# Fetching the rows of B and C three states ahead, in buffers that also take the second group's products

## The chip, the core and the metric

The kernel runs on one core of a Trainium2 chip. Five engines of that core work beside each other, each through its own queue in order: TensorE (PE in the profile, with its weight loads as PEld), VectorE (DVE), ScalarE (ACT), GpSimd (POOL) and SyncE (SP), which here only issues transfers. They meet through semaphores. The metric is the device time of one execution in microseconds. Before the change it is 2395.06 us, the median of three runs (2393.68 to 2396.68).

## The reference

4096 tokens (2 x 2048) of 256 features go through three layers, each added to its input:

```python
x = x + 0.5 * ffn(layernorm(x))      # 8 experts of 256 -> 1024 -> 256, top 2, capacity 640 per choice
x = x + mamba_block(layernorm(x))    # the block below
x = x + 0.5 * ffn(layernorm(x))      # the same experts again
```

The middle block is a state space layer and a small squared-ReLU network. Its core is a recurrence over time for 512 channels with 16 states each:

```python
xz = rmsnorm(x) @ in_proj_w.T;  x_in, z = split(xz)
u  = silu(causal_conv4(x_in));  x_dbl = u @ x_proj_w.T          # -> dt_low (64), B (16), C (16)
dt = softplus(dt_low @ dt_proj_w.T + dt_proj_b);  A = -exp(A_log)
h  = h * exp(dt_t * A) + (dt_t * u_t) * B_t                     # per step, 512 x 16 values
y  = sum over the 16 states of h * C_t
out = ((y + u * D) * silu(z)) @ out_proj_w.T
```

B and C have 16 rows each, one per state, and every channel uses the same row.

## The kernel before, in words

**Three stages.** `moe1` (to about 620 us in the profile) and `moe2` (from about 1996 us) run the two expert layers in units of 256 gathered tokens; they are matmuls with small work beside them. `mamba` lies between. The expert units that `moe1` leaves over ("b", four units) and those of the second expert layer that can start early ("c", four units) run beside the recurrence.

**The recurrence** (`recurrence`, L1345). Tokens are cut into 8 chunks of 512. Channels lie on the 128 partitions in 4 groups, which are taken in pairs (`PR = 2`). One slot k is one state s of one group c of one chunk: `order` (L1352) runs chunk, pair, state, and innermost the two groups of the pair, so there are 512 slots, and two neighbouring slots use the same row of B and the same row of C. `divmod(k, PR)` gives the state slot n and the group q (0 or 1) in it. For each slot:

- `load(n)` (L1359), once per state slot: SP fetches row s of B into `bt` (L1366) and row s of C into `ct` (L1367), each spread over all 128 partitions, 256 KB.
- `drive(k)` (L1369): POOL multiplies dt x u (`dtu`) by `bt` into `db` (L1380), three slots ahead.
- `decay(k)` (L1382): ACT computes exp(dt x A) into a PSUM bank `h`, two slots ahead.
- `scan(k)` (L1390): DVE runs the scan over 512 steps in that bank (L1396), and ACT copies the last column as the next chunk's start, `st` (L1401).
- `output(k)` (L1403), one slot later: DVE multiplies `h` by `ct` into `hc` (L1406), and PE adds it to the group's sum in PSUM through an identity matmul (L1417). The first state of a pair also adds u x D (L1411); after the last one `gate` (L1420) multiplies with silu(z).

**Buffers.** Each is 128 x 512 values of 4 bytes. There are 2 of `bt` and 4 of `ct` in pool "bc", and 4 of `db` and 5 of `hc` in pool "scan": 15 in all. A new tile waits for the last reader of the tile that had its buffer.

**Order of the rest.** All other work of the block is written as generators that yield a `Need`: modelled times on engines, a PSUM bank, a mark to wait for. `Side` plans them: after each slot, `slot` (L152) adds the slot's own times (`OWN`) to a modelled busy time of each engine and emits whichever steps fit. `AHEAD` says how far an engine's modelled time may run past that of the slot before the model moves the slot, `BEHIND` how late an engine may be and still be given another step, and `late` how long after a step its result is there. `until(mark)` (L166) emits steps, the earliest first, until a mark is set: `drive` uses it for the step sizes of a pair (mark "dt") and `load` for the rows of B and C (mark "bc").

`chunk_front` (L1147) prepares a chunk: it fetches x (L1155), normalises (`bn`, L1165), projects, convolves, computes B and C, stores them to DRAM (`bc`, L1261), from which `load` reads them, and then dt and dtu (`steps`, `log1p`, last op L1308). `chunk_tail` (L1451) finishes one: it fetches x once more as `xt` (L1459), takes ACT's `v` from it (L1480), projects out, runs the small network, stores the result to `out` (L1517) and calls `route` (L389), the routing of the second expert layer. `route` normalises (`bn`, POOL's `nmr`, ACT's `row`, L421) and stores the 512 KB of rows to one or two DRAM buffers (L429): two for the first four chunks, one for the others. All these fetches and stores are issued from SP, whose queue also carries the loads of B and C.

Of the kernel before, what the change touches and what calls it, by code (L numbers as in the profile page):

```python
# [9 lines left out]
F32 = mybir.dt.float32  # L10
# [3 lines left out]
ALU = mybir.AluOpType  # L14
# [5 lines left out]
B, T, D = 2, 2048, 256  # L20
# [13 lines left out]
RW = D + 2  # L34
# [5 lines left out]
NU_A, NU_B, NU_C, NU_D = 28, 4, 7, 25  # L40
# [34 lines left out]
class Side:  # L75
# [4 lines left out]


    OWN = {"dve": 1.8, "act": 0.88, "pe": 0.0, "pool": 1.27}
    BEHIND = {"dve": 0.6, "act": 1.2, "pe": 4.0, "pool": 4.0}
    AHEAD = {"dve": 0.0, "act": 2.0, "pe": 4.5, "pool": 4.0}
    EARLY = {"dve": 0.4, "act": 0.8, "pe": 1.0, "pool": 1.0}

    def __init__(self):
# [141 lines left out]
class Kernel:  # L229
# [156 lines left out]

        self.nc.gpsimd.tensor_tensor(out, in_, self.nhalf[:, : in_.shape[1]], ALU.pow)

    def route(self, x, t0, pool, bank, rows, pair=None):  # L389


        nc = self.nc
        n = x.shape[1]
# [24 lines left out]
        row = t("row", [P, n, RW])  # L418
        for j in range(n):
            yield Need(act=0.45)  # L420
            nc.scalar.activation(  # L421
                row[:, j, :D], x[:, j, :], AF.Identity,
                bias=nmr[:, j : j + 1], scale=rstd[:, j : j + 1],
            )

        def store(a, columns):
            for to in rows:
                at = to[t0 * P : (t0 + n) * P, columns].rearrange("(j p) d -> p j d", p=P)
                nc.sync.dma_start(out=at, in_=a)  # L429

        if pair is None:
            lg = t("lg")
        else:
            store(row[:, :, :D], slice(0, D))
            if j1 == 0:
                pair["lg"] = t("lg", [P, 2 * n, E])
            lg = pair["lg"]
# [32 lines left out]
        size, gates = n, row[:, :, D:]  # L470
        if pair is not None:
# [88 lines left out]
        at, late = t("at", W3), t("late", W3)  # L560
        nc.vector.scalar_tensor_tensor(at, best, float(PB), blk, ALU.mult, ALU.add)
        nc.vector.tensor_scalar(late, pos, float(CAP), SKIP, ALU.is_ge, ALU.mult)
        nc.vector.tensor_tensor(at, at, late, ALU.add)
        store(row if pair is None else gates, slice(0 if pair is None else D, RW))
        for j in range(0, n, size):
            yield from self.enlist(t, bank, lo[:, j : j + size], at[:, j : j + size], t0 + j)

# [579 lines left out]
    def chunk_front(self, i, pools, ch, before):  # L1147

        nc = self.nc
        pool, stp, ps, dr = pools["work"], pools["state"], pools["ps"], pools["dram"]  # L1150
        W1 = [P, TC]
        v, g, act = nc.vector, nc.gpsimd, nc.scalar
        yield Need(late=2.5, after=("b", NU_B - 1 if i == NCHUNK // 2 else -1))
        x = pool.tile([P, NJ, D], F32, tag="x", name="x")
        nc.sync.dma_start(out=x, in_=self.tiles(self.acc)[i])  # L1155

# [92 lines left out]
        NR = DTR + 2 * DS  # L1249
# [7 lines left out]
        xd = pool.tile(W1, F32, tag="xd", name="xd")[:NR, :]  # L1257
        yield Need(act=0.6, free=1, sets=("bc", i))
        act.copy(xd, xp)
        bc = ch["bc"] = dr.tile([2 * DS, TC], F32, tag="bc", name="bc")  # L1260
        nc.sync.dma_start(out=bc[:, :], in_=xd[DTR:NR, :])  # L1261


        yield self.log1p(i, pool, ch)
# [80 lines left out]
    def recurrence(self, pools, chunks, side):  # L1345

        nc = self.nc
        sp, bcp, stp = pools["scan"], pools["bc"], pools["state"]  # L1350
        W1 = [P, TC]
        order = [  # L1352
            (i, p * PR + q, s) for i in range(NCHUNK) for p in range(NP) for s in range(DS)
            for q in range(PR)
        ]
        pairs = order[::PR]
        dA, db, bt, ct, y, h, hc = {}, {}, {}, {}, {}, {}, {}

        def load(n):  # L1359
            if n < len(pairs):  # L1360
                i, _, s = pairs[n]
                side.until(("bc", i))
                bt[n] = bcp.tile(W1, F32, tag="bt", name="bt")
                ct[n] = bcp.tile(W1, F32, tag="ct", name="ct", bufs=4)
                bc = chunks[i]["bc"]
                nc.sync.dma_start(out=bt[n], in_=bc[s : s + 1, :].partition_broadcast(P))  # L1366
                nc.sync.dma_start(out=ct[n], in_=bc[DS + s : DS + s + 1, :].partition_broadcast(P))  # L1367

        def drive(k):  # L1369
            if k < len(order):  # L1370
                i, c, s = order[k]
                n, q = divmod(k, PR)
                if q == 0:
                    if s == 0:
                        side.until(("dt", NC * i + c + PR - 1))
                    if n == 0:
                        load(n)
                    load(n + 1)
                db[k] = sp.tile(W1, F32, tag="db", name="db", bufs=4)
                nc.gpsimd.tensor_tensor(db[k], chunks[i]["dtu"][c // PR][:, q, :], bt[n], ALU.mult)  # L1380

        def decay(k):  # L1382
            if k < len(order):
                i, c, s = order[k]
                dA[k] = pools["h"].tile(W1, F32, tag="h", name="h")
                nc.scalar.activation(  # L1386
                    dA[k], chunks[i]["dt"][c], AF.Exp, scale=self.A[:, c, s : s + 1]
                )

        def scan(k):  # L1390
            i, c, s = order[k]
            ch = chunks[i]
            if k % (NC * DS) == 0:
                ch["state"] = stp.tile([P, NC, DS], F32, tag="st", name="st")
            h[k] = dA.pop(k)
            nc.vector.tensor_tensor_scan(  # L1396
                h[k], h[k], db.pop(k),
                chunks[i - 1]["state"][:, c, s : s + 1] if i % (T // TC) else 0.0,
                ALU.mult, ALU.add,
            )  # L1400
            nc.scalar.copy(ch["state"][:, c, s : s + 1], h[k][:, TC - 1 :])  # L1401

        def output(k):  # L1403
            i, c, s = order[k]
            t = hc[k] = sp.tile(W1, F32, tag="hc", name="hc", bufs=5)
            nc.vector.tensor_tensor(t, h.pop(k), ct[k // PR], ALU.mult)  # L1406
            if k % (PR * DS) < PR and k >= PR:
                gate(k - PR)
            if s == 0:
                y[c] = pools["yps"].tile(W1, F32, tag="y", name="y_ps")  # L1410
                nc.tensor.matmul(  # L1411
                    y[c], lhsT=self.skip[:, c, :], rhs=chunks[i]["xc"][c], start=True, stop=False
                )
                side.did(pe=0.88)
                if k % PR == PR - 1:
                    side.mark(("begun", NP * i + c // PR))
            nc.tensor.matmul(y[c], lhsT=self.ident, rhs=hc.pop(k), start=False, stop=(s == DS - 1))  # L1417
            side.did(pe=0.88)

        def gate(k):  # L1420
            i, c, _ = order[k]
            ch = chunks[i]
            side.until(("out", i - 1))
            yc = ch["yc"][c] = pools["work"].tile(W1, F32, tag="yc", name="yc", bufs=4)
            side.until(("z", NC * i + c))
            nc.vector.tensor_tensor(yc, y[c], ch["zs"][c], ALU.mult)
            side.did(dve=0.68)
            if k % PR == PR - 1:
                side.mark(("scan", NP * i + c // PR))

        for k in range(3):
            drive(k)
        self.lone = False
        while self.lent:
            side.earliest()
        for k in range(2):
            decay(k)
        for k in range(len(order) + 1):
            if k < len(order):
                scan(k)  # L1440
                decay(k + 2)
            if k:
                output(k - 1)
            drive(k + 3)
            side.mark(("slot", k))
            side.slot()
        self.lone = True
        for k in range(len(order) - PR, len(order)):
            gate(k)

    def chunk_tail(self, i, pools, ch):  # L1451

        nc = self.nc
        pool, ps = pools["work"], pools["ps"]
        g, W1 = nc.gpsimd, [P, TC]
        y = ch["yc"]
        yield Need(late=2.5, rank=1)
        x = pool.tile([P, NJ, D], F32, tag="xt", name="xt")
        nc.sync.dma_start(out=x, in_=self.tiles(self.acc)[i])  # L1459
        yield Need(after=("scan", NP * i + NP - 1))  # L1460
# [32 lines left out]
        t = pool.tile([P, NJ], F32, tag="rs_in", name="rs_in")  # L1493
# [20 lines left out]
            yield Need(act=0.6)  # L1514
            nc.scalar.activation(hm[:, c, :], hm[:, c, :], AF.Square)
        yield from pairs(lambda c: hm[:, c, :], self.w_pr, "pr_ps", x, x)
        nc.sync.dma_start(out=self.tiles(self.out)[i], in_=x)  # L1517
        yield Need()
        half = i < NCHUNK // 2
        to = self.rows[1:] if half else self.rows[1:2]  # L1520
        if i % 2 == 0:
            self.pair = {}
        yield from self.route(x, i * NJ, pool, lambda tag: (ps, "mm"), to, self.pair)
        yield Need(sets=("routed", i))
        if i == NCHUNK // 2 - 1:
            yield self.plan_half(pools["exp"])
# [3 lines left out]
    def mamba(self):  # L1530
# [3 lines left out]
        with ExitStack() as ctx:  # L1534
# [5 lines left out]
            def aside(name, bufs):  # L1540
                tp = tc.tile_pool(name=f"mb_{name}", bufs=bufs, side="right")
                return short.enter_context(tp)

            pools = {
                "scan": aside("scan", 2),
                "bc": aside("bc", 2),
                "work": pool("work", 1),
                "exp": pool("exp", 1),
                "state": pool("state", 2),
# [105 lines left out]
```

## Time and profile before

| | us |
|---|---|
| median of three runs | 2395.06 |
| the profiled execution | 2385.7 |
| its span in the trace | 2384.0 |
| first to last slot of the recurrence | 641 to 1862 |
| in these 1221 us: PE / DVE / ACT / POOL busy | 1061 / 1075 / 734 / 911 |

The profile is one execution. Its page gives the busy time of each engine and, for forty equal slices of the span, busy shares in tenths; PEclk is the TensorE clock that was granted, as a share of full speed. Groups of instructions are named by line, engine and tile: "h<-h,st,db" of L1396 is the scan. A line of waits says which engine's instruction waited for which other one: total us, how often, the longest. A timeline line gives start, duration, engine, line, operation and, in brackets, the engine's idle time before it and what ended it. "SPq" is SP's queue; its instructions are the issues of transfers, which land some time after.

### The profile page before, as it was taken

The numbers are of one execution on the slowest core, as the hardware profiler recorded it, in microseconds if no ns is written. First come the engines' busy times: TensorE is split into PE (matmuls) and PEld (weight loads), VectorE is DVE, ScalarE is ACT, GpSimd is POOL, SyncE is SP. The second block draws the span as 40 slices with busy tenths as digits, with TensorE's granted clock in tenths as the row PEclk, the third lists the DMA queues.
The fourth block names the chain that finished last, engine by engine and source line by source line (L and its number), as shares of the span: only waits on it lengthen the run. The fifth ranks groups of instructions, "written<-read, shape, count | busy, mean of one in ns | idle before, by whom it ended". The sixth has DMA issues, their size and how long they took to land. (4 is left out here: it accounts for less than half of the span.)

```text
span 2384.0 us, 24140 instructions
## 1 busy us (share of the span) xinstructions
PE 2058.1 (86%) x7253; PEld 1309.4 (55%) x7253; DVE 1339.1 (56%) x2321; ACT 1018.7 (43%) x2316; POOL 1467.8 (62%) x1408
## 2 busy tenths in 40 slices
PE   4399999977798898997989877899888986999997
PEld 2288888864453343442434433344445665888886
DVE  6521112111287897989988898899988342111111
ACT  4122222212556666766576653676645321222221
POOL 3355555543687877877688764877767436555543
PEclk8599999998899998999999987999989998999999
DMA  8165544652264454444455434454455334565463
GB/s 265 57 223 153 155 115 115 186 156 65 66 167 121 124 139 138 126 142 113 137 133 143 128 95 135 131 143 132 114 137 157 92 95 131 187 191 152 117 192 104
DMA packets 155625, 326.14 MB, mean 137 GB/s; under 512 B 30387, under 2 KB 77340, under 8 KB 147804
## 3 DMA queue, kind: packets, MB, share of 16 engines
q1 hardware_dynamic: 115868, 174.17, 26.3%
q0 software_dynamic: 39616, 150.31, 21.3%
q8 instruction: 61, 1.00, 0.2%
q14 instruction: 80, 0.66, 0.1%
HBM read 324.86 MB, written 36.38 MB: 152 GB/s over the span
## 5 line engine op out<-in xcount | busy, mean ns | idle before, releaser
L1380 POOL TENSOR_TENSOR db<-dtu,bt 128x512 f32<-128x512 f32 x512 | 653.4, 1306 | 199.9 <-DVE h L1396 100.1
L1417 PE MATMUL y_ps<-hc,ident 128*128 128x512 f32 x1024 | 557.7, 652 | 121.6 <-DVE hc L1406 121.2
L1396 DVE TENSOR_TENSOR_SCAN h<-h,st,db 128x512 f32<-128x512 f32 x384 | 491.0, 1279 | 30.7 <-POOL db L1380 26.4
L800 ACT ACTIVATE h<-hp,w 128x256 f32<-128x256 f32 x424 | 178.0, 471 | 644.9 <-PE hp L842 584.2
L1417 PEld LDWEIGHTS y_ps<-hc,ident 128*128 128x128 f32 x1024 | 189.5, 201 | 396.0 <-DVE hc L1406 256.3
L842 PE MATMUL hp<-xbT,w 128*128 128x256 f32 x1696 | 378.0, 381 | 10.0 <-DMA w<-in_expert,widxd 3.0
L849 PE MATMUL yp<-w,h 128*128 128x256 f32 x1696 | 376.7, 380 | 0.0
L1386 ACT ACTIVATE h<-dt,A 128x512 f32<-128x512 f32 x512 | 358.9, 701 | 2.7 <-POOL dt L1306 2.3
L1406 DVE TENSOR_TENSOR hc<-h,ct 128x512 f32<-128x512 f32 x512 | 344.1, 672 | 27.2 <-ACT st L1401 27.0
L842 PEld LDWEIGHTS hp<-xbT,w 128*128 128x128 f32 x1696 | 321.5, 191 | 61.1 <-issue 7.3
L849 PEld LDWEIGHTS yp<-w,h 128*128 128x128 f32 x1696 | 319.7, 191 | 41.7
L785 DVE COPY xbT<-tp 128x512 f32<-128x512 f32 x53 | 36.7, 692 | 374.0 <-PE tp L781 374.0
L1401 ACT COPY st<-h 128x1 f32<-128x1 f32 x512 | 81.2, 159 | 352.6 <-DVE h L1396 351.6
L811 DVE TENSOR_TENSOR y<-yp,w 128x256 f32<-128x256 f32 x106 | 45.0, 425 | 288.0 <-PE yp L849 288.0
L763 POOL DMA_INDIRECT acc<-y,ids x56 | 90.3, 1612 | 152.9 <-DMA acc<-y,ids 68.8
L1396 DVE TENSOR_TENSOR_SCAN h<-h,db 128x512 f32<-128x512 f32 x128 | 156.2, 1220 | 34.6 <-POOL db L1380 31.9
L763 POOL DMA_INDIRECT out<-y,ids x50 | 80.0, 1600 | 144.1 <-DMA out<-y,ids 69.9
L196 POOL DMA_INDIRECT xb<-rows,ids x128 | 134.7, 1052 | 40.9 <-issue 33.0
L1326 PE MATMUL in_ps<-rT,w_in 128*128 128x512 f32 x256 | 126.8, 621 | 2.4 <-DVE zs L1321 1.4
L1212 PE MATMUL cv_ps<-xpad,taps 128*128 128x512 f32 x256 | 120.1, 594 | 1.3 <-DVE zs L1321 0.8
L842 PE MATMUL e_hp<-e_xT,w 128*128 128x256 f32 x352 | 90.7, 408 | 13.6 <-DVE e_y L948 8.0
L842 PEld LDWEIGHTS e_hp<-e_xT,w 128*128 128x128 f32 x352 | 72.2, 208 | 38.2 <-issue 11.3
(318 smaller groups left out, 2366.8 us busy)
## 6 DMA issues: line engine op xcount, KB each, us to landing
bt<-bc SPq DMA_DIRECT2D x256, 256.0 KB, 3.7
ct<-bc SPq DMA_DIRECT2D x256, 256.0 KB, 4.4
rows<-row SPq DMA_DIRECT2D x12, 512.0 KB, 3.3
w<-in_expert SPq DMA_DIRECT2D x2, 2304.0 KB
x<-in_x SPq DMA_DIRECT2D x8, 512.0 KB, 4.6
acc<-x SPq DMA_DIRECT2D x8, 512.0 KB, 5.2
xt<-acc SPq DMA_DIRECT2D x8, 512.0 KB, 5.9
x<-acc SPq DMA_DIRECT2D x8, 512.0 KB, 4.2
```

The lines of the kernel that those rows point to most:

```text
L196: self.nc.gpsimd.indirect_dma_start(out=out, out_offset=None, in_=src, in_offset=bass.IndirectOffsetOnAxis(ap=idx, axis=0), bounds_check=l ...
L763: self.nc.gpsimd.indirect_dma_start(out=dst, out_offset=bass.IndirectOffsetOnAxis(ap=ids, axis=0), in_=y, in_offset=None, bounds_check=las ...
L800: nc.scalar.activation(h[:, f + q, :], hp[:, q, :], AF.Relu, bias=b1[:, f + q : f + q + 1])
L842: self.nc.tensor.matmul(hp[:, q, :], lhsT=w1[:, k, (f + q) * P : (f + q + 1) * P], rhs=xT[:, k, :], start=(k == 0), stop=(k == ND - 1),)
L849: self.nc.tensor.matmul(yp, lhsT=h[:, f, j * P : (j + 1) * P], rhs=w2[:, f, :], start=(f == 0), stop=(f == NF - 1),)
L1212: nc.tensor.matmul(cv[c], lhsT=self.taps[:, c, k, :], rhs=xpad[c][:, k : k + TC], start=(k == 0), stop=(k == DC - 1),)
L1326: self.nc.tensor.matmul(mp, lhsT=self.w_in[:, k, m * P : (m + 1) * P], rhs=rT[:, k, :], start=(k == 0), stop=(k == ND - 1),)
L1380: nc.gpsimd.tensor_tensor(db[k], chunks[i]["dtu"][c // PR][:, q, :], bt[n], ALU.mult)
L1386: nc.scalar.activation(dA[k], chunks[i]["dt"][c], AF.Exp, scale=self.A[:, c, s : s + 1])
L1396: nc.vector.tensor_tensor_scan(h[k], h[k], db.pop(k), chunks[i - 1]["state"][:, c, s : s + 1] if i % (T // TC) else 0.0, ALU.mult, ALU.add,)
L1406: nc.vector.tensor_tensor(t, h.pop(k), ct[k // PR], ALU.mult)
L1417: nc.tensor.matmul(y[c], lhsT=self.ident, rhs=hc.pop(k), start=False, stop=(s == DS - 1))
```

## The change

The rows of B and C are loaded three state slots ahead (`load` is called in the main loop, for the first three before it), POOL's products are made five slots ahead, and both have other buffers: 4 of `bt` and 4 of `ct`, now in pool "scan", 3 of `db`, 4 of `hc`. The product of the second group (q = 1) is written in place over its own row: `db` over `bt`, and `hc` over `ct`. The sum is 15 buffers as before. The planner's allowances for POOL become 6 and 7 us; the results of the two fetches of x count as there 7.0 us after them, in place of 2.5. The stores of `bc`, of the routed rows and of `out` are issued from ACT's queue; that of `out` moves into `route`, behind the row activations, ahead of the row stores. The store of the gates stays on SP.

```diff
-    BEHIND = {"dve": 0.6, "act": 1.2, "pe": 4.0, "pool": 4.0}
-    AHEAD = {"dve": 0.0, "act": 2.0, "pe": 4.5, "pool": 4.0}
+    BEHIND = {"dve": 0.6, "act": 1.2, "pe": 4.0, "pool": 6.0}
+    AHEAD = {"dve": 0.0, "act": 2.0, "pe": 4.5, "pool": 7.0}
...
-    def route(self, x, t0, pool, bank, rows, pair=None):
+    def route(self, x, t0, pool, bank, rows, pair=None, out=None):
...
-        def store(a, columns):
+        if out is not None:
+            nc.scalar.dma_start(out=out, in_=x)
+
+        def store(queue, a, columns):
             for to in rows:
                 at = to[t0 * P : (t0 + n) * P, columns].rearrange("(j p) d -> p j d", p=P)
-                nc.sync.dma_start(out=at, in_=a)
+                queue.dma_start(out=at, in_=a)
...
-            store(row[:, :, :D], slice(0, D))
+            store(nc.scalar, row[:, :, :D], slice(0, D))
...
-        store(row if pair is None else gates, slice(0 if pair is None else D, RW))
+        store(nc.sync, row if pair is None else gates, slice(0 if pair is None else D, RW))
...
-        yield Need(late=2.5, after=("b", NU_B - 1 if i == NCHUNK // 2 else -1))
+        yield Need(late=7.0, after=("b", NU_B - 1 if i == NCHUNK // 2 else -1))
...
-        nc.sync.dma_start(out=bc[:, :], in_=xd[DTR:NR, :])
+        act.dma_start(out=bc[:, :], in_=xd[DTR:NR, :])
...
-                bt[n] = bcp.tile(W1, F32, tag="bt", name="bt")
-                ct[n] = bcp.tile(W1, F32, tag="ct", name="ct", bufs=4)
+                bt[n] = sp.tile(W1, F32, tag="bt", name="bt", bufs=4)
+                ct[n] = sp.tile(W1, F32, tag="ct", name="ct", bufs=4)
...
-                if q == 0:
-                    if s == 0:
-                        side.until(("dt", NC * i + c + PR - 1))
-                    if n == 0:
-                        load(n)
-                    load(n + 1)
-                db[k] = sp.tile(W1, F32, tag="db", name="db", bufs=4)
+                if q == 0 and s == 0:
+                    side.until(("dt", NC * i + c + PR - 1))
+
+                db[k] = bt[n] if q == PR - 1 else sp.tile(W1, F32, tag="db", name="db", bufs=3)
                 nc.gpsimd.tensor_tensor(db[k], chunks[i]["dtu"][c // PR][:, q, :], bt[n], ALU.mult)
...
-            t = hc[k] = sp.tile(W1, F32, tag="hc", name="hc", bufs=5)
-            nc.vector.tensor_tensor(t, h.pop(k), ct[k // PR], ALU.mult)
+            b = ct[k // PR]
+            t = hc[k] = b if k % PR == PR - 1 else sp.tile(W1, F32, tag="hc", name="hc", bufs=4)
+            nc.vector.tensor_tensor(t, h.pop(k), b, ALU.mult)
...
-        for k in range(3):
+        for n in range(3):
+            load(n)
+        for k in range(5):
             drive(k)
...
-            drive(k + 3)
+            drive(k + 5)
+            if k % PR == 0:
+                load(k // PR + 3)
...
-        yield Need(late=2.5, rank=1)
+        yield Need(late=7.0, rank=1)
...
-        nc.sync.dma_start(out=self.tiles(self.out)[i], in_=x)
         yield Need()
...
-        yield from self.route(x, i * NJ, pool, lambda tag: (ps, "mm"), to, self.pair)
+        out = self.tiles(self.out)[i]
+        yield from self.route(x, i * NJ, pool, lambda tag: (ps, "mm"), to, self.pair, out)
...
-                "bc": aside("bc", 2),
```

More of the change, by code (lines that the diff above doesn't have):

```diff
@@ L1349, in recurrence @@
         nc = self.nc
-        sp, bcp, stp = pools["scan"], pools["bc"], pools["state"]
+        sp, stp = pools["scan"], pools["state"]
         W1 = [P, TC]
```

## The prediction

> **What bounds the kernel now.** First the page's overview: the span with each engine's busy share, then the forty slices.
>
> ```profile
> span 2384.0 us, 24140 instructions
> ...
> PE   4399999977798898997989877899888986999997
> ...
> DVE  6521112111287897989988898899988342111111
> ACT  4122222212556666766576653676645321222221
> POOL 3355555543687877877688764877767436555543
> PEclk8599999998899998999999987999989998999999
> ```
>
> Outside slices 11 to 31 the two expert stages run, where PE is full and DVE nearly idle; the change touches neither. Inside, DVE, PE and POOL are all busy and none is full. Next the busy time of each engine from the first state slot to the last, 641 to 1862 us:
>
> ```profile
> 641.00:1862.00 1221.00, 1061.04 (x2764) 498.69 (x2765) 1075.29 (x1424) 734.46 (x1674) 911.21 (x858) 0.93 0.48 132
> ```
>
> The columns are PE, PEld, DVE, ACT, POOL, clock, DMA share, GB/s. DVE is the fullest, 1075 of 1221 us, so the stage cannot go below about 1075 while DVE's work stays, and 146 us of DVE idleness is all that can be won. What ended that idleness, from the waits of DVE in that window, longest first:
>
> ```profile
> DVE h L1396 <- POOL db L1380: 58.2, 30, 21.8
> DVE hc L1406 <- ACT st L1401: 27.0, 16, 4.9
> DVE bn L1165 <- DMA x<-acc: 16.5, 6, 5.4
> DVE v L1475 <- PE out_ps L1470: 10.5, 8, 3.6
> DVE e_y L948 <- PE e_yp L849: 10.4, 4, 4.1
> DVE zs L1321 <- ACT tz L1318: 10.1, 10, 1.8
> ```
>
> The 21.8 is the wait for the very first state, mostly ahead of the window; 36.4 of the first row is left. Then who held POOL and the loads, from POOL's waits, and from the timeline one stretch of SP's queue and POOL (idle time before an instruction in brackets):
>
> ```profile
> POOL db L1380 <- DVE h L1396: 100.1, 99, 4.2
> POOL db L1380 <- DMA bt<-bc: 74.4, 59, 5.8
> ```
> ```profile
> 1231.75 0.92 SPq L429 DMA_DIRECT2D rows<-row  x2
> 1232.76 1.18 SPq L1366 DMA_DIRECT2D bt<-bc  x1
> 1234.04 1.20 SPq L1367 DMA_DIRECT2D ct<-bc  x1
> ```
> ```profile
> 1242.34 1.27 POOL L1380 TENSOR_TENSOR db<-dtu,bt 128x512 f32<-128x512 f32 x1 [5.76 <-DMA bt<-bc]
> ```
>
> Two 512 KB row stores go ahead of a 256 KB load on one queue, and the product that needs the load comes 8.4 us after the load's issue ends; the median load lands in 3.7. The fourth piece is ACT, held by a fetch, with DVE behind it:
>
> ```profile
> 939.36 1.58 ACT L1480 ACTIVATE v<-xt,nmr,rstd 128x256 f32<-128x256 f32 x3 [6.49 <-DMA xt<-acc]
> 940.85 0.14 ACT L1401 COPY st<-h 128x1 f32<-128x1 f32 x1
> ```
> ```profile
> 941.01 0.69 DVE L1406 TENSOR_TENSOR hc<-h,ct 128x512 f32<-128x512 f32 x1 [4.78 <-ACT st L1401]
> ```
>
> DVE's product hc starts only after ACT has copied the same state's last column, so whatever blocks ACT's in-order queue for longer than a scan blocks DVE.
>
> **Part 1, the lead of POOL.** A slot (scan and hc) takes 1.78 us where nothing interferes (scans start at 1850.44, 1852.22, 1854.00) and 2.38 on average (1221 / 512). Before, db[k] writes the buffer of db[k-4]: from the end of that scan (1.28) to scan k are 4 x 1.78 - 1.28 = 5.8 us, less the product's own 1.28: POOL may be 4.6 us late (7.0 at average slots). Afterwards the tightest tie is the load: bt[n] writes over the product of state slot 2n-7, so it starts after that scan, needs 0.3 to issue and 3.7 to land, then 1.28 of product: 7 x 1.78 - 1.28 - 4.0 - 1.28 = 5.9 us (10.1 at average slots). The lead grows by 1.3 to 3.1 us, less than "five for three" says. DVE's waits for db over half a microsecond are 23, 34.1 us together; with 1.3 us more cover 23.7 of it goes, with 3.1 us 33.0. I take 28, in between; below, 0 (if POOL's lateness is a chain of inputs, next part), above, 36. Besides, a late POOL recovers faster: it no longer waits for a load that its own previous product released. The 74.4 us become waits for DVE and cost nothing. The same 512 products and 512 loads are issued. In place writing is free: POOL's in-place row (L1304) has a median of 1.270 us, against 1.282 for db; DVE's in-place row (L1475) 0.687 against 0.672 for hc, at 256 products +4 us at the very worst, taken as 0 since that row reads PSUM as hc does.
>
> **Part 2, what is moved behind it.** Two more products stand ahead of each piece of side work on POOL. If POOL is late these are 2 x 1.28 = 2.6 us later for whoever waits: ACT's row normalisations (18.3 us of waits in the whole trace) and the gathers of the expert units. Planner allowances of 6 and 7 us in place of 4 and 4 are meant to place consumers accordingly. Also the step sizes of a chunk must be ready two slots sooner. That matters: counting scans, the last dtu product of a chunk's first pair comes at slots 127, 191, 253, 319 and 445 where 125, 189, 253, 317 and 445 are the deadlines, so at five of seven chunk borders the planner empties its chains by force, and there ACT's four row activations fall into one slot (DVE waits of 3.5 us at 923, 4.86 at 1367). Two slots earlier means a fuller burst: I take 1 us at five borders, 5 us; bounds 0 (larger allowance lets the chain run ahead) and 10.
>
> **Part 3, later consumption of x and xt.** 7.0 in place of 2.5: 4.5 us more before bn (DVE) and v (ACT) are placed. Of the 16.5 us of bn waits only what exceeds 4.5 stays (0.9): 15.6 gone. Of the two stalls of hc behind xt, 4.78 at 941 and 3.06 at 1434, 0.3 stays: 7.5 gone. Bounds 10 and 24. The fronts are not hurt by starting bn later: bn comes at slots 34, 116, 178, 239, 309, 362 and then waits for z.
>
> **Part 4, stores on ACT's queue.** Off SP: 8 out, 12 row and 8 bc stores; the gate stores stay. What they held back on SP is the bt case above, which part 1 covers. On ACT they cost issue time, which this trace shows only on SP: 0.39, 0.46 and 0.32 us, and up to 1.74 for a load issued behind two row stores. A chunk's route puts two or three of them right after ACT's row activations: 0.9 to 1.9 us, of which some 0.57 (ACT's wait for tp there) hides. With st behind them, seven routes and seven bc stores make 2 to 9 us of DVE: 5. Below nothing, if ACT has slack there; far above, by POOL's indirect DMAs, 1.0 to 1.6 us each: 28 x 1.6 = 45 us. I take the SP rows as nearest, being the same instruction. At the end, out of chunk 6 is issued after its rows (about 1872.6 in place of 1860.6), and xt of chunk 7 writes the buffer that it reads: xt starts some 4.5 us after, not at 1873.0. v at 1882.3 was 5 us clear of its landing: 2 us, bounds 0 and 4.5. SP's own new wait: a ct load now waits for PE's sum over the old product, and the next bt, x, xt and list stores queue behind it; PE may be 1.8 us behind before bt feels it and 7 us before POOL does.
>
> The Trainium skill, "DMA: Bandwidth & Descriptors", section "Issuing engines are not separate DMA queues", says that initiating DMAs on several engines only saves sequencer time, since all run on the same 16 engines. By that, part 4 is worth nothing to the loads (the bytes still precede them) and is all cost. The 5.76 us above is with stores on the load's own queue, so no row here decides it.
>
> **Part 5, what is late next.** PE is busy 1061 us in the stage at a clock of 0.93, and DVE's rows that wait on PE or ACT side chains (v, e_y, zs twice, xt, xc: 10.5, 10.4, 10.1, 5.8, 7.1, 4.3) make 48 us. A DVE that arrives sooner waits longer there: 0 to 24 us, half of them again; I take 8, since PE still has 160 us idle.
>
> **Sum.** 28 + 15.6 + 7.5 = 51.1 won; 5 + 5 + 2 + 8 = 20 lost; 31 us net. The profiled execution took 2385.7 us (2384.0 of span and 1.7 around it), 9.4 under the median 2395.06, so 2354.7 for such an execution and about 2364 for the median.
>
> **Rivals.** *ACT becomes the hold-up (slower).* Place: the route's two or three stores, 1 to 1.5 MB at once. If ACT's queue blocks until the descriptors find room, as the load behind the row stores hints (1.74 for 0.38), and its stall goes through st to hc one for one, the gain of 51.1 - 15 = 36 is gone at 36 / 7 = 5.1 us per route; at 8 us it is 7 x 8 - 36 = 20 us slower, 2415. Against it: SP took 0.92 for the two stores themselves. *Given back.* The same waits return at PE and the forced bursts (24 + 10 in place of 8 + 5): 51 - 24 - 10 - 5 - 2 = 10 us, 2385. For it: where DVE is full (1600 to 1660 us: 20.0, 20.0, 18.7 of 20) PE is at 19.8, 19.1, 20.0. *No lead at all.* POOL's lateness at the borders is the chain xd, dt, Ln, dtu, which no buffer shortens; db gives 5, stores and fetches cancel: within 5 us, 2395. *More.* All listed targets and part of the border stalls, 36 + 24 + 15 (of ACT's), nothing lost: 75 us, 2320.
>
> **How the numbers follow.** About 0.2%, 5 us, is what a measurement here can tell from no change. Likeliest case 0.45 (2340 to 2378); more 0.13; given back 0.20 (0.17 clearly faster, 0.03 within); no lead 0.06; ACT 0.16 (0.01 within). Faster 0.45 + 0.13 + 0.17 = 0.75; within 0.03 + 0.06 + 0.01 = 0.10; slower 0.15. For 8 in 10 the range runs from 2325 (most of "more") to 2405 (half of the slower case).
>
> **What would show it.** DVE waits on db under 12 us in the stage; POOL's waits on bt under 15; bn waits on x near 0; no ACT wait on xt with an hc wait after it; ACT DMA issues near 0.4 us each. Wrong if hc's waits on st exceed 40 us, if ACT shows long gaps behind the route's stores, if SP's ct loads wait long for PE, or if the last border (1862 to 1996) stretches by more than 5 us.

## The result and the profile after

| | before | after | after / before, 95% interval |
|---|---|---|---|
| median of four runs, us | 2394.37 (2392.88 to 2396.68) | 2415.04 (2411.48 to 2418.81) | 1.0086 [1.0067, 1.0104] |
| the profiled execution | 2385.7 | 2411.5 | |
| its span | 2384.0 | 2409.7 | |
| start of the first scan | 643.0 | 641.8 | |
| first to last scan ("the stage") | 1215.9 | 1235.1 | |
| from the last scan to the end ("the tail") | 525.2 | 532.8 | |

The change makes the kernel 0.86% slower, about 20.7 us, where 31 us of gain were forecast. Between the two profiled executions 19.2 us are lost in the stage and 7.6 in the tail, and 1.2 are won ahead of it. The mean granted clock of the two is 0.935 before and 0.934 after, so the clock is not the reason. The page's overview of the kernel after:

```profile
span 2409.7 us, 24259 instructions
...
PE   4399999978797897987989887888769894999997
...
DVE  6521112111487897989986998988978223111111
ACT  3122222212555756655665664666625331222221
POOL 2355555443787867777695874887757334555543
```

DVE still has the most work in the stage, and none has noticeably more of it than before (POOL 913 us against 911, the others less). The busy time from the first scan to the last, kernel after (columns as before: PE, PEld, DVE, ACT, POOL, clock, DMA share, GB/s):

```profile
641.77:1876.90 1235.13, 1050.71 (x2757) 490.63 (x2758) 1064.81 (x1421) 727.14 (x1666) 912.83 (x858) 0.94 0.42 129
```

So the loss is waiting: from the first scan to the last DVE stands idle for 170 us (1235.1 - 1064.8), where it was 143 (1215.9 - 1072.8). What ended DVE's idle time in that window, kernel after:

```profile
DVE hc L1407 <- ACT st L1401: 36.2, 13, 9.1
DVE v L1480 <- PE out_ps L1475: 32.8, 12, 6.8
DVE h L1396 <- POOL db L1380: 27.2, 9, 12.5
DVE ct L1407 <- ACT st L1401: 15.4, 13, 2.6
DVE zs L1324 <- ACT tz L1321: 14.3, 16, 1.8
DVE xc L1228 <- ACT th L1224: 13.2, 4, 6.3
...
DVE bn L1168 <- DMA x<-acc: 3.6, 2, 2.2
```

The waits that the change was forecast to shorten are shorter: the scan's wait for `db` is 27.2 us, of which 12.5 is the first state's, so 14.7, with 1.6 more for the products made over `bt`, in place of 36.4, and `bn` waits 3.6 in place of 16.5. In their place stand waits for side results: all rows on `st` grow from 34.3 to 54.5 (the first and fourth row here, and some short ones), `v` on PE from 10.5 to 32.8, `xc` from 4.3 to 13.2. Then who held POOL, and who held SP's queue, kernel after:

```profile
POOL db L1380 <- DMA bt<-bc: 150.8, 67, 10.2
POOL db L1380 <- DVE h L1396: 26.6, 8, 9.5
```
```profile
SPq L1370 <- PE y_ps L1418: 844.1, 243, 16.3
```

POOL now waits twice as long for rows of B, 150.8 us against 74.4, although they are ordered three states ahead. And 243 of the 256 loads of C stand at the head of SP's queue until PE has added the old product that lies in their buffer. The total of 844 says little by itself, since SP waits for somebody in every kernel (737 us for POOL in the one before); what matters is who comes next in that queue. One stretch of the timeline of the kernel after, DVE, PE, SP and POOL in turn:

```profile
858.76 0.67 DVE L1407 TENSOR_TENSOR ct<-h,ct 128x512 f32<-128x512 f32 x1
```
```profile
859.91 1.88 PE L1215 MATMUL cv_ps<-xpad,taps 128*128 128x512 f32 x4
861.63 1.88 PE L1513 MATMUL fc_ps<-rvT,w_fc 128*128 128x512 f32 x4
863.35 1.02 PE L1412 MATMUL y_ps<-xc,skip 128*128 128x512 f32 x2
864.20 1.02 PE L1418 MATMUL y_ps<-ct,ident 128*128 128x512 f32 x2
```
```profile
865.26 0.32 SPq L1370 DMA_DIRECT2D ct<-bc  x1
865.67 0.38 SPq L1369 DMA_DIRECT2D bt<-bc  x1
```
```profile
870.40 1.28 POOL L1380 TENSOR_TENSOR db<-dtu,bt 128x512 f32<-128x512 f32 x1 [6.87 <-DMA bt<-bc]
```

DVE has written its product by 859.43. PE has convolution and network matmuls first and adds the product from 864.20 to 865.22. 0.04 us later the load of C is issued, behind it the next load of B, and 4.7 us after that POOL's product can start, having stood idle for 6.87 us. DVE can feel such a delay by a detour. The kernel after, ACT and DVE at a border between chunks:

```profile
776.13 0.63 ACT L1305 ACTIVATE dt<-dt 128x512 f32<-128x512 f32 x1 [6.62 <-POOL dtu L1301]
776.67 0.14 ACT L1401 COPY st<-h 128x1 f32<-128x1 f32 x1
```
```profile
776.85 0.69 DVE L1407 TENSOR_TENSOR hc<-h,ct 128x512 f32<-128x512 f32 x1 [9.12 <-ACT st L1401]
```

POOL reaches the step-size work late (it had waited 3.00 us for `bt` at 758.77 and 1.01 for a scatter at 766.69), ACT's logarithm waits 6.62 us for POOL's product, the copy `st` waits behind the logarithm, and DVE's `hc` waits 9.12 us for `st`. How much of the 54.5 us on `st` comes about in this way can't be told from one border.

### The profile page after: what moved, and what is told of

Read it like the earlier page. It is cut to its first block, busy times and chain, and to the rows that moved or that the text cites. A ratio compares the mean times of both kernels' runs of the same rounds, so it can differ in the third digit from the quotient of the medians.

```text
span 2409.7 us, 24259 instructions
## 1 busy us (share of the span) xinstructions
PE 2051.6 (85%) x7253; PEld 1309.5 (54%) x7253; DVE 1331.6 (55%) x2321; ACT 1011.3 (42%) x2310; POOL 1471.9 (61%) x1408
## 5 line engine op out<-in xcount | busy, mean ns | idle before, releaser
L1380 POOL TENSOR_TENSOR db<-dtu,bt 128x512 f32<-128x512 f32 x256 | 333.4, 1302 | 191.9 <-DMA bt<-bc 150.8
L1418 PE MATMUL y_ps<-hc,ident 128*128 128x512 f32 x512 | 288.6, 647 | 74.1 <-DVE hc L1407 73.9
L1380 POOL TENSOR_TENSOR bt<-dtu,bt 128x512 f32<-128x512 f32 x256 | 331.3, 1294 | 15.9
L1418 PE MATMUL y_ps<-ct,ident 128*128 128x512 f32 x512 | 284.2, 638 | 55.2 <-DVE ct L1407 55.0
L1396 DVE TENSOR_TENSOR_SCAN h<-h,st,db 128x512 f32<-128x512 f32 x192 | 245.5, 1279 | 16.0 <-POOL db L1380 13.0
L1396 DVE TENSOR_TENSOR_SCAN h<-h,st,bt 128x512 f32<-128x512 f32 x192 | 245.5, 1278 | 5.8 <-ACT h L1386 2.6
L1418 PEld LDWEIGHTS y_ps<-hc,ident 128*128 128x128 f32 x512 | 93.7, 199 | 215.8 <-DVE hc L1407 139.4
L1418 PEld LDWEIGHTS y_ps<-ct,ident 128*128 128x128 f32 x512 | 92.5, 197 | 188.4 <-DVE ct L1407 117.3
L1407 DVE TENSOR_TENSOR hc<-h,ct 128x512 f32<-128x512 f32 x256 | 172.2, 673 | 36.3 <-ACT st L1401 36.2
L1407 DVE TENSOR_TENSOR ct<-h,ct 128x512 f32<-128x512 f32 x256 | 172.2, 673 | 15.5 <-ACT st L1401 15.4
```

Of the source, the lines that this page charges most:

```text
L1396: nc.vector.tensor_tensor_scan(h[k], h[k], db.pop(k), chunks[i - 1]["state"][:, c, s : s + 1] if i % (T // TC) else 0.0, ALU.mult, ALU.add,)
L1407: nc.vector.tensor_tensor(t, h.pop(k), b, ALU.mult)
```

## The experiments

Four theories were set against each other in the first four kernels. **R**: SP, held by PE ahead of each load of C, brings the rows of B late. **P**: the new planner numbers force more steps (by the order of the program, 183 steps in the recurrence are emitted by a forced `until`, 66 before). **S**: the stores hold ACT up. **D**: the step sizes are due two slots sooner. Each ratio is that of the medians against runs of the kernel before on the same chip; where two of these kernels are compared, it is by their ratios.

**The planner's numbers put back**

```diff
-    BEHIND = {"dve": 0.6, "act": 1.2, "pe": 4.0, "pool": 6.0}
-    AHEAD = {"dve": 0.0, "act": 2.0, "pe": 4.5, "pool": 7.0}
+    BEHIND = {"dve": 0.6, "act": 1.2, "pe": 4.0, "pool": 4.0}
+    AHEAD = {"dve": 0.0, "act": 2.0, "pe": 4.5, "pool": 4.0}
...
-        yield Need(late=7.0, ...)
+        yield Need(late=2.5, ...)      # both fetches of x
```

> The changed kernel with the planner's numbers of before (POOL 4 and 4, x after 2.5); buffers, lead of five slots and the stores on ACT stay. Theory P (the planner): the loss is made by side steps that the planner emits by force at a deadline, inside one slot; in the recurrence it emits 66 such steps in the kernel before, 183 in the changed one, 94 here. DVE stands idle some 70 us at those places in the changed kernel and some 20 before, so this gives back 35 to 45 us: 2370 to 2382, faster than before (2394). Theory S (ACT is held up by the stores): unchanged stores, so 2410 to 2418. Theory R (SP waits for PE before each load of C, and B's next row waits behind it): 2410 to 2418. Theory D (the deadline of the step sizes two slots sooner does it): 2403 to 2415.

Measured: 2443.91 us, 1.0224 [1.0202, 1.0246]. With half the forced steps (94) the kernel is 1.38% slower than the changed one, 33 us by the ratios (29 between the medians), so the numbers are not what costs; they make the loss smaller. None of the four theories had this: P expected 2370 to 2382 us, the others 2403 to 2418. POOL and DVE of this kernel, from their waits:

```profile
POOL db L1380 <- DMA bt<-bc: 184.1, 81, 11.9
```
```profile
DVE bn L1168 <- DMA x<-acc: 30.6, 6, 6.3
```

The fetches of x stand in the same held queue, and with a result due after 2.5 us `bn` waits 30.6 us for them. Besides, the first scan comes 12.5 us later than in the changed kernel (654.3 against 641.8).

**The planner's numbers alone, in the kernel before**

```diff
-    BEHIND = {..., "pool": 4.0}
-    AHEAD = {..., "pool": 4.0}
+    BEHIND = {..., "pool": 6.0}
+    AHEAD = {..., "pool": 7.0}
...
-        yield Need(late=2.5, ...)
+        yield Need(late=7.0, ...)
```

> The kernel before with nothing of the change but the planner's numbers (POOL 6 and 7, x after 7.0): 172 forced steps in place of 66. Theory P: the loss without the gain of the buffers, 2394 + 35 to 50 = 2430 to 2445. Theories S, R and D: nothing here of what they name; the fetches of x stop holding DVE and ACT, so 2375 to 2396.

Measured: 2398.71 us, 1.0025 [1.0011, 1.0038]: the new numbers, with 172 forced steps, cost 6 us. P had expected 2430 to 2445, the other theories 2375 to 2396, just under the result. `bn` waits 2.4 us in place of 16.5, as forecast, but `v` waits 27.3 us for PE in place of 10.5, and the tail grows from 525.2 to 534.0 us, without any store moved. P falls with these two runs.

**The stores back on SP**

```diff
-            store(nc.scalar, row[:, :, :D], slice(0, D))
+            store(nc.sync, row[:, :, :D], slice(0, D))
...
-        act.dma_start(out=bc[:, :], in_=xd[DTR:NR, :])
+        nc.sync.dma_start(out=bc[:, :], in_=xd[DTR:NR, :])
...
+        nc.sync.dma_start(out=self.tiles(self.out)[i], in_=x)
         yield Need()
```

> The changed kernel with all stores issued from SP again, out ahead of the route; the order of all other instructions is the same. Theory S: 2395 or less. Theories P, R and D: within 6 us of 2415; a little slower if rows of B wait behind the row stores again.

Measured: 2419.3 us, 1.0121 [1.0096, 1.0146], against 1.0086 [1.0067, 1.0104] with the stores on ACT. Not faster, so S falls. Whether the move to ACT is worth the 4 us between the medians isn't told apart, as the intervals overlap. The waits are those of the changed kernel: POOL 152.3 us for `bt`, SP 813.8 for PE.

**The second group's C product in a buffer of its own**

```diff
-            t = hc[k] = b if k % PR == PR - 1 else sp.tile(W1, F32, tag="hc", name="hc", bufs=4)
+            t = hc[k] = sp.tile(W1, F32, tag="hc", name="hc", bufs=4)
```

> The changed kernel, but the second group's product with C goes to one of the 4 hc buffers as the first group's does, not over the row of C: a load of C then waits for DVE and no longer for PE. SP's waits for PE (844 us) go. Theory R: POOL's waits for rows of B fall from 151 us to under 90 and the time by 10 us or more, to 2405 or less. Theories P, S and D: POOL's waits fall, the time stays within 6 us of 2415, since DVE waits for POOL's products only 15 us in the recurrence of the changed kernel; a few us more if 4 hc buffers for all slots make DVE wait for PE.

Measured: 2382.04 us, 0.9962 [0.9951, 0.9974]. One line, the same 15 buffers, and 1.24% less than the changed kernel, 30 us by the ratios; it is faster than both kernels. SP and POOL of it:

```profile
SPq L1370 <- DVE hc L1407: 636.6, 235, 18.5
```
```profile
POOL db L1380 <- DMA bt<-bc: 87.5, 55, 7.2
```

No load of C waits for PE's additions any more, POOL's wait for `bt` falls from 150.8 to 87.5, and DVE's waits on `st` from 54.5 to 35.7. This is inside what R expected, and S and D fall with it: the stores on ACT and the deadline two slots sooner are still there, and the loss is gone. But the edit also takes the products of both groups through four `hc` buffers, and that could have helped by itself.

The next four kernels were made for what was then open. **B**: the four buffers helped, not SP's freedom. **P2**: forced steps are a second cause beside R. **N**: the planner's numbers only shift stalls. **K**: the later due time of x only covers fetches that SP issues late.

**The C loads ordered one state later, the product left in place**

```diff
-                ct[n] = sp.tile(W1, F32, tag="ct", name="ct", bufs=4)
...
+        def load_c(n):
+            if n < len(pairs):
+                i, _, s = pairs[n]
+                ct[n] = sp.tile(W1, F32, tag="ct", name="ct", bufs=4)
...
+        for n in range(2):
+            load_c(n)
...
                 load(k // PR + 3)
+                load_c(k // PR + 2)
```

> The changed kernel, but a row of C is fetched two states ahead in place of three: its load is issued one state slot later, so it wants the PE sum of a slot that is three slots old, not one. The product over the row of C, the order of all other work and the planner's 183 forced steps stay. Theory R (SP is held by PE ahead of each load of C, B's next row waits behind it, POOL is late, ACT waits for POOL's side results and DVE for ACT): SP's waits for PE fall from 844 us to under 200, the time to 2375 to 2390, as with the product apart (2382). Theory B (four hc buffers in turn, not the released SP, made that kernel faster): 2410 to 2418.

Measured: 2394.37 us, 0.9993 [0.9984, 1.0002]. The product still lies over the row of C; only the load that must wait for PE comes a state later, when PE is done more often. Of the loss, 0.93% comes back (22 us by ratio). That is less than R had expected (2375 to 2390 us, SP's waits for PE under 200), and far more than B had (2410 to 2418). SP and POOL:

```profile
SPq L1375 <- PE y_ps L1423: 260.9, 148, 7.0
```
```profile
POOL db L1385 <- DMA bt<-bc: 77.8, 54, 7.0
```

Two edits that have nothing in common but SP's wait for PE both bring POOL's wait for `bt` back to about 80 us, and one gives back all of the 30 us, the other three quarters. The issues of the loads show the link between: in the changed kernel a load of B is issued a median of 1.4 us after the end of the scan that frees its buffer, over 2 us after it in 108 of 252 cases, and both here and with the product apart a median of 0.03 us after it. R stands. The 7 us by ratio by which the separate buffer is better than the later load may be the rest of the PE wait, or B; that isn't told apart.

**The other way round: only the tie, added to the kernel before**

```diff
-            t = hc[k] = sp.tile(W1, F32, tag="hc", name="hc", bufs=5)
-            nc.vector.tensor_tensor(t, h.pop(k), ct[k // PR], ALU.mult)
+            b = ct[k // PR]
+            t = hc[k] = b if k % PR == PR - 1 else sp.tile(W1, F32, tag="hc", name="hc", bufs=5)
+            nc.vector.tensor_tensor(t, h.pop(k), b, ALU.mult)
```

> The kernel before with one edit of the change alone: the second group's product is written over its row of C. Lead of three slots, two buffers of B, five of hc and planner stay. Theory R: SP waits for PE ahead of each load of C here too, and B's next row behind it has less time to spare than in the changed kernel, so 15 to 50 us slower: 2409 to 2445. If the wait is hidden: 2389 to 2399.

Measured: 2406.24 us, 1.0046 [1.003, 1.0062]: 11 us slower, below the 15 that R expected at least. SP waits 393 us (163 times) for PE, half of what it does in the changed kernel, and POOL 108.2 us for `bt` in place of 74.4. In the kernel before, B is fetched one state ahead and the loads wait for POOL's products anyway, so there is less time to lose; that reason is argued. The sign and the path to POOL are as R has them, and B can't explain it: this edit leaves the five `hc` buffers to half of the products, and is slower. The way on to DVE differs: its waits on `st` don't rise (33.1 against 34.3 us); those of `bn` for x do, from 16.5 to 22.3, and those on `tz` from 10.1 to 15.7.

**Fewer forced steps, with the product apart**

```diff
-    BEHIND = {"dve": 0.6, "act": 1.2, "pe": 4.0, "pool": 6.0}
-    AHEAD = {"dve": 0.0, "act": 2.0, "pe": 4.5, "pool": 7.0}
+    BEHIND = {"dve": 0.6, "act": 1.2, "pe": 4.0, "pool": 8.0}
+    AHEAD = {"dve": 0.0, "act": 2.0, "pe": 4.5, "pool": 2.5}
```

> The changed kernel with the product with C apart (2382), and planner numbers for POOL of 8 and 2.5 in place of 6 and 7 (x stays 7.0), with which 40 steps are forced in the recurrence in place of 183. Theory P2 (forced steps are a second cause, worth about 40 us of DVE's idleness at seven deadlines, once SP is free): 2345 to 2368. Theory N (the numbers only shift stalls about): 2376 to 2390.

Measured: 2399.1 us, 1.0015 [1.0002, 1.0028], 0.53% over the same kernel with 183 forced steps, though only 40 are left. `v` waits less for PE (19.2 us) but DVE waits 49.7 us on `st`. P2 falls: forced steps as such are not what costs here. N, with 2376 to 2390, misses as well.

**The old planner numbers, with the product apart**

```diff
-    BEHIND = {..., "pool": 6.0}
-    AHEAD = {..., "pool": 7.0}
+    BEHIND = {..., "pool": 4.0}
+    AHEAD = {..., "pool": 4.0}
...
-        yield Need(late=7.0, ...)
+        yield Need(late=2.5, ...)
```

> The product with C apart, and the planner's numbers of before (4, 4, 2.5): 94 forced steps. With SP held by PE these numbers cost 29 us against the changed ones (2444 to 2415). Theory K (the later due time of x only covers fetches that SP issues late, so the cost goes when SP is free): 2372 to 2386. If the numbers matter in themselves: 2395 to 2411. Theory P2: 94 for 183 steps forced, 2360 to 2372.

Measured: 2398.04 us, 1.0005 [0.9996, 1.0014]: with SP free the new numbers are worth 0.43%, 10 us, where 1.38% lay between the same two settings with SP held by PE. In the profile the stage begins 15.7 us later (655.6 against 639.9) with the old numbers and the tail is 5.1 us shorter (526.5 against 531.6). K misses, and so does P2; the expectation that the numbers matter in themselves (2395 to 2411) is met. Of the 15.7 us, 6 are there already when the first row of B is fetched (620.5 against 614.5); after that the first scan waits 21.8 us for its product in place of 11.7. Why is not shown.

The last four kernels ask where the rest of the forecast gain went. **G**: PE takes it back. **H**: it is lost to the bunching of planned work. **A**: ACT's copy of the state carries the stalls to DVE.

**Half the convolution left out, product apart and kernel before**

Of the four taps of the causal convolution only the first two are multiplied, so the result is not the reference's.

```diff
-            for k in range(k0, k0 + 2):
-                nc.tensor.matmul(... start=(k == 0), stop=(k == DC - 1))
+            k = k0 // 2
+            nc.tensor.matmul(... start=(k == 0), stop=(k == 1))
```

> The kernel with the product with C apart (2382, ratio 0.996), with two of the four taps of the convolution left out, so its output is not the reference's: 128 of PE's 256 conv matmuls go, some 55 us of PE's busy time in the stage; the order of everything else stays. Theory G (what the lead and the later fetch win, 43 us of DVE's waits, is given back because PE, at 87% busy in order, cannot follow a faster DVE): 2335 to 2360, and the gap to the kernel before with the same taps left out grows to 20 us or more. Theory H (the gain is lost to how the side steps are bunched, whatever PE's load): 2368 to 2382, and the gap stays about 10.

> The kernel before with the same two taps left out (output not the reference's). Theory G: PE is not what holds DVE here, so 2378 to 2392. Theory H: about 10 us above the run with the product apart, 2378 to 2392 as well; the two theories differ in the gap.

Measured: 2369.31 us, 0.9901 [0.9878, 0.9925] with the product apart, and 2386.74 us, 0.997 [0.9956, 0.9985] in the kernel before. The same work taken off PE gives 0.61% there and 0.30% here; the distance between the two kernels grows from 0.38% to 0.69%, from 9 to 17 us. That would fit PE taking back a part of what the lead wins. But PE's own time did not fall alike: from 1052 to 1003 us in the stage with the product apart, from 1058 to 1032 in the kernel before, at granted clocks of 0.94 and 0.95 there and of 0.93 and 0.92 here. So part of the wider distance may be the clock, and PE's share is not shown. And `v` waits 30.9 us for PE with half the convolution and 31.4 with all of it: it is not PE's total work that this row waits for. G, which had expected 2335 to 2360 us and a distance of 20 or more, is too much; the time lies in H's 2368 to 2382, but the distance is not its 10.

**ACT's copy of the state two slots later, product apart and kernel before**

```diff
-            nc.scalar.copy(ch["state"][:, c, s : s + 1], h[k][:, TC - 1 :])
+        def keep(k):
+            if 0 <= k < len(order):
+                i, c, s = order[k]
+                nc.scalar.copy(chunks[i]["state"][:, c, s : s + 1], h.pop(k)[:, TC - 1 :])
...
+                keep(k - 2)
```

> The product with C apart, and ACT's copy of a state's last column two slots later, so that DVE's product no longer has an ACT copy ahead of it that may stand behind ACT's side work. DVE waits 36 us for that copy in the stage. Theory A (ACT's in-order queue is the channel by which late POOL and PE results reach DVE): these waits go, some return at the decays, which have two slots to spare; 20 to 30 us less, 2352 to 2365. If the waits only move to the decays: 2376 to 2386.

> The kernel before with the same later copy and nothing else. It has 34 us of DVE's waits for that copy. Theory A: 2366 to 2378. Otherwise 2388 to 2398.

Measured: 2384.58 us, 0.9965 [0.995, 0.9981] with the product apart, 2394.32 us, 1.0003 [0.9985, 1.0021] in the kernel before: nothing, twice, as the expectations had it for the case that the waits only move. `hc` no longer waits for a copy that has just been queued, and DVE's waits on `st` fall from 35.7 to 16.8 us, but its scan now waits 25.0 us for ACT's exponentials where it waited 8.4:

```profile
DVE h L1396 <- ACT h L1386: 25.0, 17, 6.2
```

When ACT is late, DVE waits for it at the next thing that it needs from ACT. The rows on `st` name the place where the lateness shows, not its cause. A falls; H is neither shown nor excluded.

## Why the prediction was wrong

**The step that failed** is the last sentence of part 4, SP's own new wait, priced at nothing: "PE may be 1.8 us behind before bt feels it and 7 us before POOL does". The mechanism was named there, with the right place and the right queue, and its condition was listed under what would make the forecast wrong ("if SP's ct loads wait long for PE"). What is missing is how far behind PE is. The trace of before shows it: from the end of DVE's product of a second group (L1406) to the end of PE's second matmul on it (L1417) it takes a median of 2.9 us over the 256 products, more than 1.8 in 186 of them, and more than 7 in 3. Nor was 1.8 us to spare: in the same trace the scan that frees the next row's buffer ends a median of 1.2 us after the product. In the changed kernel 220 of 252 loads of B are issued more than 0.3 us after that scan, with the product apart one. The 7 us for POOL would hold if POOL had nothing else that makes it late, but it is busy 913 us of the stage, and a lead of 5.9 us has to cover PE's lag and POOL's side work together. That last piece is argued; the price is measured: 30 us by taking the tie away, 22 by moving the load, against a step taken as 0. Of the signs that were listed for being wrong three came: the products wait 51.6 us for `st` (36.2 + 15.4), the loads of C wait for PE, and the end is 7.6 us longer.

That step alone does not close the account. Without it the kernel gains 9 us (0.38%) where 31 were forecast; most of the rest is the term of part 5, the waits that were to grow by 8 us and grew by 43.

**Part 1** is right once SP is free. Forecast were 28 us off the waits for `db`; with the product apart they fall from 36.4 to 9.3 (8.3 and 1.0 for products made over `bt`), 27 us, and with it in place to 16.3. In-place writing itself is free, as taken: `db` over `bt` takes 1294 ns on average and into its own buffer 1302, both `hc` forms 673. What the part said of POOL failed: it was to wait for `bt` under 15 us, and waits 87.5 even with the product apart; the waits for DVE went instead, from 100.1 to 33.0. The load, not the scan, is what POOL runs into, but late enough that DVE rarely notices.

**Part 2** (5 us for a fuller burst at five borders) can't be read off alone. With the product apart, plans with 40, 94 and 183 forced steps give ratios of 1.0015, 1.0005 and 0.9962, so their number is no measure of a loss.

**Part 3.** The 15.6 us of `bn` are nearly right: 3.6 us of the 16.5 are left, and under 1 with the product apart. ACT's waits for `xt` fall from 16.9 to 5.0 and 1.3 us. The 7.5 us behind them don't show as a gain, since the waits on `st` are 35.7 us with the product apart, and were 34.3. What the part did not see is the start: with the old numbers and the new buffers the first scan comes 12.5 and 15.7 us later (with the product in place and apart), so much of the numbers' 10 us lies ahead of the stage.

**Part 4, the stores.** ACT's issues take 0.44 us for `out` and 0.94 for two row stores, as on SP, as forecast. The 5 us priced for them can't be found: with the stores back on SP the kernel isn't faster. The Trainium skill's rule that a second issuing engine only saves the time of issuing ("DMA: Bandwidth & Descriptors", "Issuing engines are not separate DMA queues") fits that run. The 2 us at the end were 7.6, but not for the reason given: every kernel with the change's planner numbers has a tail of 530 to 535 us, also the one that leaves all stores where they were (534.0), and every one with the old numbers 524 to 528. Why the numbers do this is not shown.

**Part 5** was mis-sized: 8 us (0 to 24) for what PE and ACT's chains take back. With the product apart DVE's waits on `out_ps`, `e_yp`, `tz`, `pr_ps`, `th` and for ACT's `h` rise from 10.5 + 10.4 + 10.1 + 6.7 + 4.3 + 2.4 = 44.4 to 31.4 + 11.5 + 18.2 + 6.2 + 12.1 + 8.4 = 87.8 us: 43 us, nearly all of the 27 + 16 won (by the prediction's own rows, from 48 to 80). These rows of the kernel with the product apart:

```profile
DVE v L1480 <- PE out_ps L1475: 31.4, 11, 6.3
DVE h L1396 <- POOL db L1380: 20.0, 6, 11.7
DVE zs L1324 <- ACT tz L1321: 18.2, 17, 3.0
DVE xc L1228 <- ACT th L1224: 12.1, 5, 4.8
```

(11.7 of the second row is the first state's.) Without the first state's wait, which lies ahead of the first scan, DVE's waits in the stage are 143 us against 139 before: on the whole these two profiles show no waiting won (that of before lies 8.7 us under its median, so in a usual execution it may be that much). The profiled stage is 7.1 us shorter all the same (1208.8 against 1215.9), since DVE's busy time in it is 10.7 us smaller (1062.1 against 1072.8). Most of that is small rows of the routing that took less time, `cand` 1.3 us in place of 8.5 and `room` 8.2 in place of 14.4; why is not shown. Some of the returned waiting comes with the planner's numbers: alone they raise the wait on `out_ps` to 27.3, and putting them back lowers it to 20.7, as `bn`'s come back. Some may be PE's work, which the runs with half the convolution don't settle. What sets the rest isn't known: fewer forced steps bring the six rows down to 66 us but those on `st` up to 49.7, a later copy moves the waits on, and neither kernel is faster.

**Rivals.** 2415 us is to the microsecond what the ACT rival gave, but that is chance, for its mechanism did not occur: ACT's stores take a microsecond at most, and moving them back changes nothing for the better. The hold-up of the changed kernel is not in the queue that got the stores, ACT's, but in the one that lost them, SP's. "Given back" is the rival that the kernel with the product apart comes nearest to, 2382 against 2385.

**The profiled execution.** The one of before, 2385.7, lies below all four of its timed runs, 8.7 us under their median, those of the changed kernel and of the one with the product apart 3.6 and 0.0 under theirs. So the difference between the profiles shows a loss 5 us larger and a gain 6 us smaller than the medians do.

## What to carry to other kernels

Writing a product in place of its operand saves a buffer, but it hands the buffer's release from the engine that reads the operand to the engine that reads the product. Before doing so, read in the trace how late that engine is (here PE's median of 2.9 us was enough), and list what is queued behind the load that will wait for it: loads with different releasers want different places in the order, or the one with the slow releaser wants a later one. And a wait taken from an engine that is not alone at its limit can come back under another name, as 43 us did here, so count the sum of its waits, not the row that is gone.

## What the runs showed of the hardware

- A load issued from SP waits in order with those behind it, free or not: with 243 loads waiting for PE, a load of B is issued a median of 1.4 us after its own buffer is free, and POOL's wait for its rows is 150.8 us; without them it is 0.03 us, and 87.5. The landing times known (some 65 of 256 of each kind) differ little: medians of 3.7 and 3.4 us from issue for B and C there, 3.3 and 3.3 without, 3.7 and 4.4 in the kernel before.
- Of the 512 KB stores the traces have few landings, and these overlap. The row stores took 3.2, 3.3 and 5.3 us in the kernel before and 3.6, 5.8 and 7.5 in the kernel with the stores put back, both from SP, and 6.6 and 7.6 from ACT in the changed one. The `out` stores took 4.5 us from SP (one, kernel before), 2.9 and 3.8 from SP (stores put back) and 2.9 to 3.2 from ACT (three). So a difference between the two queues is not shown.
- DVE's product of a bank of PSUM waits for ACT's copy of one column from the same bank (27.0 us, 16 times in the kernel before), though both only read. The Trainium skill's "PSUM — Partial Sum Buffer", section "PSUM bank collisions raise a hardware error", says that two engines must not access one bank in the same partitions at a time, reads included; no run here tried it without any wait. With the copy moved behind the product, the copy waits for the product (145 times, 175 us of ACT's idle time) in place of the other way round.
